# One DMA queue for loads and stores in turns, with 12 slots instead of 23

## The chip, the cores and the metric

The kernel runs on one core of one Trainium2 chip. The metric is the device time of one execution in microseconds (us). Engines are named as in the profile: PE is TensorE, DVE is VectorE, ACT is ScalarE, POOL is GpSimd, SP is SyncE; SPq and ACTq are the DMA queues that SyncE and ScalarE issue to.

## The reference

There are 128 samples. Each sample `b` is a matrix of 128 channels by 1024 time steps in float32, and it has a subject, a number from 0 to 7. Each subject has a 128 x 128 weight matrix. The sample is multiplied by the matrix of its subject, and the product is added to the sample:

```python
def reference(x, itok_B_0_7, L0_cond_weights):     # x: (128, 128, 1024), weights: (8, 128, 128)
    w = L0_cond_weights[itok_B_0_7]                # one (128, 128) matrix a sample
    return x + jnp.einsum('bct,bcd->bdt', x, w)
```

The samples are 67.1 MB that have to come in and 67.1 MB that have to go out.

## The kernel before

Samples are worked on in pairs (`G = 2`), so there are `NT = 64` pairs, each 1 MB. A pair lives in one slot of on-chip memory, `xs[k]`, with 128 channels on the partitions and 2 x 1024 values on each. There are `SLOTS = 23` slots; pair `i` uses slot `i % SLOTS`. The product is added to the sample in place, so a slot is loaded, changed and stored, and is free for another pair when the store has landed.

Each engine has its own list of instructions, and semaphores hold the lists together:

- SyncE first loads all weights (`w_all`), then issues the loads of all pairs in order. A load of a pair is two calls of `transfer`, one a sample (0.5 MB each), both counted by `s_load[k]`. For a slot's second and later uses it first waits for the store of the pair that was in it (`s_store[k]`). For the first use of the slots it keeps at most `LEAD = 3` pairs in flight, by waiting for the load of three pairs earlier.
- GpSimd reads the subject of a sample and copies its weight matrix out of `w_all` into one of four buffers (L158).
- TensorE waits for the load, and multiplies each sample in two halves of 512 columns into one of four PSUM buffers (L164). Three matmuls of zeros come ahead (L111).
- VectorE adds the PSUM buffer to the sample in its slot (L174), and counts `s_added`.
- ScalarE waits until both samples of a pair are added, and issues the pair's store, one transfer of 1 MB, counted by `s_store[k]`. It issues no arithmetic.

So loads and stores go through two hardware queues: `QUEUES` names one for SyncE and one for ScalarE. `transfer` is the helper that issues on either; its line is 53, which is why loads and stores carry the same line in the profile. In each queue the transfers start in the order of issue; between the queues nothing sets an order but the semaphores. At the end SyncE waits for the stores of the last `SLOTS` pairs.

Of the kernel before, what the change touches and what calls it, by code (L numbers as in the profile page):

```python
# [1 line left out]

# [4 lines left out]

F32 = mybir.dt.float32
I32 = mybir.dt.int32
ALU = mybir.AluOpType


G = 2

N = 512  # L30

SLOTS = 23

W_SLOTS = 4
P_SLOTS = 4
DMA = 16

LEAD = 3

IDLE = 3  # L40

ROWS = 4
QUEUES = {mybir.EngineType.SP: "qSPDynamicHW", mybir.EngineType.Activation: "qActDynamicHW"}


def transfer(nc, engine, out, in_):

    later, nc._always_lower_symbolic_ap = nc._always_lower_symbolic_ap, False  # L50
    ins, outs = engine.lower_ap_dma(in_), engine.lower_ap_dma(out)
    nc._always_lower_symbolic_ap = later
    return engine.add_instruction(  # L53
        mybir.InstDMACopy(
            name=nc.get_next_instruction_name(),
            engine=engine.engine,
            ins=ins,
            outs=outs,
            mode="Copy",
            cce_op=ALU.bypass,  # L60
            queue=QUEUES[engine.engine],
        )
    )


@with_exitstack
def kernel(
    ctx: ExitStack,
    tc: tile.TileContext,
    x: bass.AP,  # L70
    subjects: bass.AP,
    weights: bass.AP,
    out: bass.AP,
):
    nc = tc.nc
    B, C, T = x.shape
    S, _, D = weights.shape
    NT = B // G

    def sbuf(name, *shape, dtype=F32):  # L80
        return ctx.enter_context(nc.sbuf_tensor(name, list(shape), dtype)).ap()

    given, near, wrap, index = (
        sbuf(name, 1, B, dtype=I32) for name in ("given", "near", "wrap", "index")
    )
    w_all = sbuf("w_all", C, S, D)
    ws = [sbuf(f"w{i}", C, 1, D) for i in range(W_SLOTS)]
    zeros = sbuf("zeros", C, N)
    xs = [sbuf(f"x{i}", C, G, T) for i in range(SLOTS)]
    ps = [  # L90
        ctx.enter_context(nc.psum_tensor(f"ps{i}", [D, T], F32)).ap() for i in range(P_SLOTS)
    ]

    s_given = tc.alloc_semaphore("s_given")
    s_wall = tc.alloc_semaphore("s_wall")
    s_index = tc.alloc_semaphore("s_index")
    s_zeros = tc.alloc_semaphore("s_zeros")
    s_copied = tc.alloc_semaphore("s_copied")
    s_product = tc.alloc_semaphore("s_product")
    s_added = tc.alloc_semaphore("s_added")  # L100
    s_load = [tc.alloc_semaphore(f"s_load{i}") for i in range(SLOTS)]
    s_store = [tc.alloc_semaphore(f"s_store{i}") for i in range(SLOTS)]

    with tc.tile_critical():  # L104

        nc.scalar.dma_start(given, subjects.rearrange("(o b) -> o b", o=1)).then_inc(s_given, DMA)

        nc.vector.memset(zeros, 0.0).then_inc(s_zeros, 1)  # L108
        nc.tensor.wait_ge(s_zeros, 1)
        for _ in range(IDLE):  # L110
            nc.tensor.matmul(  # L111
                ps[P_SLOTS - 1][:, :N], zeros[:, :D], zeros, start=True, stop=True
            )

        nc.vector.wait_ge(s_given, DMA)
        nc.vector.tensor_scalar(near, given, -S, S - 1, ALU.max, ALU.min).then_inc(s_index, 1)  # L118
        nc.vector.wait_ge(s_index, 1)
        nc.vector.tensor_scalar(wrap, near, 0, S, ALU.is_lt, ALU.mult).then_inc(s_index, 1)  # L120
        nc.vector.wait_ge(s_index, 2)
        nc.vector.tensor_tensor(index, near, wrap, ALU.add).then_inc(s_index, 1)  # L122
        nc.gpsimd.wait_ge(s_index, 3)

        nc.sync.dma_start(w_all, weights.rearrange("s c d -> c s d")).then_inc(s_wall, DMA)  # L127
        for i in range(NT):
            k, turn = i % SLOTS, i // SLOTS
            if turn:  # L130
                nc.sync.wait_ge(s_store[k], DMA * turn)
            elif i >= LEAD:
                nc.sync.wait_ge(s_load[k - LEAD], DMA * G)
            for g in range(G):
                transfer(
                    nc,
                    nc.sync,
                    xs[k][:, g, :],
                    x[i * G + g].rearrange("(a r) t -> a (r t)", r=ROWS),
                ).then_inc(s_load[k], DMA)  # L140

        nc.gpsimd.wait_ge(s_wall, DMA)
        for i in range(NT):
            k, turn = i % SLOTS, i // SLOTS
            nc.tensor.wait_ge(s_load[k], DMA * G * (turn + 1))
            for g in range(G):
                b = i * G + g
                s = nc.values_load(
                    index[0:1, b : b + 1],
                    engines=[mybir.EngineType.Pool],  # L150
                    min_val=0,
                    max_val=S - 1,
                    skip_runtime_bounds_check_because="the index is clamped on the chip above",
                )
                w, p = ws[b % W_SLOTS], ps[b % P_SLOTS]
                if b >= W_SLOTS:
                    nc.gpsimd.wait_ge(s_product, b - W_SLOTS + 1)
                nc.gpsimd.tensor_copy(w, w_all[:, bass.ds(s, 1), :]).then_inc(s_copied, 1)  # L158

                nc.tensor.wait_ge(s_copied, b + 1)  # L160
                if b >= P_SLOTS:
                    nc.tensor.wait_ge(s_added, b - P_SLOTS + 1)
                for t in range(0, T, N):
                    mm = nc.tensor.matmul(  # L164
                        p[:, t : t + N],
                        w[:, 0, :],
                        xs[k][:, g, t : t + N],
                        start=True,
                        stop=True,
                    )  # L170
                mm.then_inc(s_product, 1)

                nc.vector.wait_ge(s_product, b + 1)
                nc.vector.tensor_tensor(xs[k][:, g, :], p, xs[k][:, g, :], ALU.add).then_inc(  # L174
                    s_added, 1
                )
            nc.scalar.wait_ge(s_added, (i + 1) * G)
            transfer(
                nc,
                nc.scalar,  # L180
                out[i * G : (i + 1) * G].rearrange("g d t -> d g t"),
                xs[k].rearrange("d (o g) t -> d o (g t)", o=1),
            ).then_inc(s_store[k], DMA)


        for i in range(NT - SLOTS, NT):
            nc.sync.wait_ge(s_store[i % SLOTS], DMA * (i // SLOTS + 1))


# [1 line left out]
_INS = ["x", "itok_B_0_7", "L0_cond_weights"]  # L191
_OUTS = [((128, 128, 1024), "float32")]


# [20 lines left out]
```

## Time and profile before

| | |
|---|---|
| median of 6 runs | 328.06 us (327.55 to 328.2) |
| the profiled execution | 328.06 us, its span 326.1 us |
| DMA: bytes, mean rate over the span | 134.86 MB, 414 GB/s |
| TensorE, VectorE, GpSimd busy | 74%, 48%, 12% of the span |
| mean granted TensorE clock | 0.925 |
| one load transfer, issue to landing | 11.8 us (median) |
| one store transfer, issue to landing | 41.5 us (median) |

The span is the part of the execution that the trace shows; the rest of the time lies around it. The strips of the page cut the span into 40 slices of 8.15 us, and each digit is the busy share of a slice in tenths. DMA is the mean of the core's 16 DMA engines, GB/s what they moved. A time "to landing" runs from the issue of a transfer until its semaphore is complete, and so has in it all the time for which the transfer waited in its queue.

### The profile page before, as it was taken

What the parts mean: (1) busy time and instruction counts of PE and PEld (TensorE: products, weight loads), DVE (VectorE), ACT (ScalarE), POOL (GpSimd) and SP (SyncE); (2) the same over time, 40 slices, a digit from 0 to 9 for tenths busy, and PEclk for the clock granted to TensorE, in tenths of its full rate; (3) what the DMA queues carried; (4) which work ended last, traced back from release to release, by engine and by line L of the source; (5) the groups of instructions that cost most, each with busy time, mean ns of one, the idle gap of its engine ahead of it and who ended that gap; (6) DMA issues with size and microseconds to landing.
All of it is one profiled execution on the core that took longest, in us unless ns stands there. A gap on an engine that the chain in (4) does not pass through costs nothing.

```text
span 326.1 us, 1941 instructions
## 1 busy us (share of the span) xinstructions
PE 241.5 (74%) x518; PEld 95.2 (29%) x518; DVE 158.0 (48%) x132; POOL 37.8 (12%) x132
## 2 busy tenths in 40 slices
PE   7999988988989888998898898898796876000000
PEld 2444433333333333333333333333232332000000
DVE  1666766556555565665565565666365445000000
POOL 1111111111111111111111111111011110000000
PEclk9999999999999999999999999999799999755555
DMA  7999999999999999999999999999999999999993
GB/s 267 408 414 420 422 426 423 426 424 427 425 421 427 423 425 423 425 428 423 427 424 419 425 424 428 422 419 426 423 438 423 419 423 427 425 427 425 427 425 166
DMA packets 16411, 134.86 MB, mean 414 GB/s; under 512 B 3089, under 2 KB 4114, under 8 KB 4114
## 3 DMA queue, kind: packets, MB, share of 16 engines
q1 hardware_dynamic: 7184, 67.64, 49.7%
q10 hardware_dynamic: 9218, 67.11, 49.1%
q8 instruction: 4, 0.07, 0.1%
q14 instruction: 5, 0.04, 0.0%
HBM read 67.63 MB, written 67.11 MB: 413 GB/s over the span
## 4 chain that ended last, share of the span: by engine, by line
DMA 45%; SPq 24%; another core or an unknown queue 14%; PE 1%; issue 1%; DVE 0%
DMA x<-in_x_dram 30%; SPq L53 23%; DMA out_dram<-x 15%; PE ps L164 1%; DVE x L174 0%; SPq L127 0%; SPq L211 0%; SPq L104 0%
## 5 line engine op out<-in xcount | busy, mean ns | idle before, releaser
L164 PE MATMUL ps<-x,w 128*128 128x512 f32 x512 | 236.0, 607 | 32.5 <-DMA x<-in_x_dram 32.2
L174 DVE TENSOR_TENSOR x<-ps,x 128x1024 f32<-128x1024 f32 x128 | 156.8, 1225 | 117.2 <-PE ps L164 117.2
L164 PEld LDWEIGHTS ps<-x,w 128*128 128x128 f32 x512 | 93.4, 191 | 175.9 <-issue 96.6
L158 POOL COPY w<-w_all 128x128 f32 x128 | 37.6, 294 | 228.1 <-PE ps L164 222.5
L111 PE MATMUL ps<-zeros 128*128 128x512 f32 x6 | 5.5, 1088 | 1.7 <-DVE zeros L108 1.7
L111 PEld LDWEIGHTS ps<-zeros 128*128 128x128 f32 x6 | 1.8, 328 | 3.7 <-issue 2.1
L108 DVE MEMSET zeros<- 128x512 f32 x1 | 0.5, 485 | 1.1 <-SPq L104 1.1
L118 DVE TENSOR_SCALAR near<-given 1x128 int32<-1x128 int32 x1 | 0.2, 215 | 0.6 <-DMA given<-in_itok_B_dram 0.6
L122 DVE CUSTOM_DVE_ANT_0 index<-near,wrap 1x256 uint16<-1x256 uint16 x1 | 0.3, 281 | 0.0
L120 DVE TENSOR_SCALAR wrap<-near 1x128 int32<-1x128 int32 x1 | 0.2, 216 | 0.0
L202 POOL MEMSET const-float32-0.0<- 128x1 f32 x1 | 0.1, 98 | 0.2 <-issue 0.2
L202 POOL MEMSET const-bfloat16-1.0<- 128x1 bf16 x1 | 0.1, 101 | 0.0
L202 POOL MEMSET const-uint8-127<- 128x1 uint8 x1 | 0.1, 101 | 0.0
L202 POOL MEMSET const-float32-1.0<- 128x1 f32 x1 | 0.1, 98 | 0.0
## 6 DMA issues: line engine op xcount, KB each, us to landing
x<-in_x_dram SPq DMA_DIRECT2D x128, 512.0 KB, 11.8
out_dram<-x ACTq DMA_DIRECT2D x64, 1024.0 KB, 41.5
w_all<-in_L_cond_weights_dram SPq DMA_DIRECT2D x1, 512.0 KB, 3.9
given<-in_itok_B_dram ACTq DMA_DIRECT2D x1, 0.5 KB
```

Source lines behind the costliest of these rows:

```text
L53: return engine.add_instruction(mybir.InstDMACopy(name=nc.get_next_instruction_name(), engine=engine.engine, ins=ins, outs=outs, mode="Cop ...
L108: nc.vector.memset(zeros, 0.0).then_inc(s_zeros, 1)
L111: nc.tensor.matmul(ps[P_SLOTS - 1][:, :N], zeros[:, :D], zeros, start=True, stop=True)
L118: nc.vector.tensor_scalar(near, given, -S, S - 1, ALU.max, ALU.min).then_inc(s_index, 1)
L120: nc.vector.tensor_scalar(wrap, near, 0, S, ALU.is_lt, ALU.mult).then_inc(s_index, 1)
L122: nc.vector.tensor_tensor(index, near, wrap, ALU.add).then_inc(s_index, 1)
L158: nc.gpsimd.tensor_copy(w, w_all[:, bass.ds(s, 1), :]).then_inc(s_copied, 1)
L164: mm = nc.tensor.matmul(p[:, t : t + N], w[:, 0, :], xs[k][:, g, t : t + N], start=True, stop=True,)
L174: nc.vector.tensor_tensor(xs[k][:, g, :], p, xs[k][:, g, :], ALU.add).then_inc(s_added, 1)
L202: nc = _bacc.Bacc("TRN2", target_bir_lowering=False, num_devices=1)
```

## The change

All loads and stores of samples are issued by SyncE on its one queue. The order is written out: the loads of the first six pairs, then in turns the load of pair `i + 6` and the store of pair `i`. `SLOTS` falls from 23 to 12, and `LEAD`, now the distance between load and store in this order, is 6 where the old `LEAD` was 3. The old wait that kept three loads in flight goes. Before a store SyncE waits for `s_added`, as ScalarE did. ScalarE keeps only the load of the subjects. The instructions of TensorE, VectorE and GpSimd stay as they are, in the same order.

```diff
-SLOTS = 23
+SLOTS = 12
...
-LEAD = 3
+LEAD = 6
...
-QUEUES = {mybir.EngineType.SP: "qSPDynamicHW", mybir.EngineType.Activation: "qActDynamicHW"}
+QUEUES = {mybir.EngineType.SP: "qSPDynamicHW"}
...
         nc.sync.dma_start(w_all, weights.rearrange("s c d -> c s d")).then_inc(s_wall, DMA)
-        for i in range(NT):
+
+        def load(i):
             k, turn = i % SLOTS, i // SLOTS
             if turn:
                 nc.sync.wait_ge(s_store[k], DMA * turn)
-            elif i >= LEAD:
-                nc.sync.wait_ge(s_load[k - LEAD], DMA * G)
             for g in range(G):
                 transfer(
                     nc,
                     nc.sync,
                     xs[k][:, g, :],
                     x[i * G + g].rearrange("(a r) t -> a (r t)", r=ROWS),
                 ).then_inc(s_load[k], DMA)
+
+        def store(i):
+            k = i % SLOTS
+            nc.sync.wait_ge(s_added, (i + 1) * G)
+            transfer(
+                nc,
+                nc.sync,
+                out[i * G : (i + 1) * G].rearrange("g d t -> d g t"),
+                xs[k].rearrange("d (o g) t -> d o (g t)", o=1),
+            ).then_inc(s_store[k], DMA)
+
+        for i in range(LEAD):
+            load(i)
+        for i in range(NT):
+            if i + LEAD < NT:
+                load(i + LEAD)
+            store(i)
...
-            nc.scalar.wait_ge(s_added, (i + 1) * G)
-            transfer(
-                nc,
-                nc.scalar,
-                out[i * G : (i + 1) * G].rearrange("g d t -> d g t"),
-                xs[k].rearrange("d (o g) t -> d o (g t)", o=1),
-            ).then_inc(s_store[k], DMA)
```

## The prediction

> **What bounds the kernel now.** I read the strips of the page first, since they show each resource over the whole span.
>
> ```profile
> PE   7999988988989888998898898898796876000000
> DVE  1666766556555565665565565666365445000000
> DMA  7999999999999999999999999999999999999993
> GB/s 267 408 414 420 422 426 423 426 424 427 425 421 427 423 425 423 425 428 423 427 424 419 425 424 428 422 419 426 423 438 423 419 423 427 425 427 425 427 425 166
> q1 hardware_dynamic: 7184, 67.64, 49.7%
> q10 hardware_dynamic: 9218, 67.11, 49.1%
> ```
>
> The DMA strip is full from the second slice to the last but one, and goes on for six slices in which TensorE and VectorE do nothing. q1 (SyncE's queue, the loads) and q10 (ScalarE's, the stores) together use 98.8% of 16 engines' span. So the bytes through the 16 DMA engines set the time: 134.86 MB. The change leaves the bytes as they are, so it can act in only two ways: it lets the engines run empty, or it changes the rate at which they move bytes.
>
> For the rate I asked for the busy time by stretches. After the times stand PE, PEld, DVE and POOL busy, then TensorE's clock, the DMA share and GB/s.
>
> ```profile
> 8.00:10.00 2.00, 2.00 (x5) 0.96 (x6) 0.08 (x1) 0.00 (x0) 1.00 1.02 426
> 10.00:12.50 2.50, 2.50 (x7) 1.14 (x6) 2.01 (x2) 0.59 (x2) 1.00 1.01 413
> 12.50:15.00 2.50, 2.50 (x7) 1.07 (x6) 1.59 (x2) 0.29 (x1) 1.00 0.98 400
> 15.00:17.50 2.50, 2.50 (x8) 1.06 (x7) 1.93 (x2) 0.59 (x2) 1.00 0.99 351
> 30.00:150.00 120.00, 107.44 (x235) 42.12 (x234) 71.21 (x60) 17.06 (x59) 1.00 1.01 425
> 220.00:270.00 50.00, 39.74 (x84) 15.67 (x83) 25.50 (x21) 5.88 (x20) 0.97 1.01 425
> 280.00:320.00 40.00, 0.00 (x0) 0.00 (x0) 0.00 (x0) 0.00 (x0) 0.51 1.01 426
> 320.00:324.50 4.50, 0.00 (x0) 0.00 (x0) 0.00 (x0) 0.00 (x0) 0.50 0.26 109
> ```
>
> Three regimes are to be seen. Up to about 17 us only loads move: first at 426 GB/s, then 413, then 400, with the engines nearly as busy. From 30 to 270 us loads and stores move together at 425. From 280 us only stores move, through one queue, at 426. So one queue alone can fill the engines when it carries stores; when it carries loads, it starts as fast and then falls.
>
> Last, the issuing side: how long an issue holds its engine (min, median, max in ns), and the landing of stores in the last stretch, where only they run.
>
> ```profile
> L53 SPq DMA_DIRECT2D x<-in_x_dram x128: 471/595/4167, 1.5 to 264.0; - x128
> L53 ACTq DMA_DIRECT2D out_dram<-x x64: 546/4311/8979, 12.9 to 301.8; - x64
> out_dram<-x ACTq DMA_DIRECT2D x10, 1024.0 KB, 22.6
> ```
>
> The median store issue holds ScalarE 4.3 us against a minimum of 0.55: the queue is full and the issue waits for room. 22.6 us to landing at 426 GB/s is 9.6 MB, so a queue holds some 9 stores. For the loads, between 90 and 145 us, the view of DMA issues gives 32.5 us to landing while q1 has 60.4% and q10 40.3% of the engines: 32.5 us x 424 GB/s x 0.6 = 8.3 MB.
>
> **The change part by part.** The profiled execution took 328.06 us, which is also the median of the runs, with a span of 326.1; 1.96 us lie around the span and I leave them. "L" below is the load of a slot (two transfers, 1.049 MB), "S" its store.
>
> Issue time. SyncE issues 128 loads and now 64 stores too: 128 x 0.595 + 64 x 0.546 = 111 us of 326, so SyncE has 215 us to spare, and it costs nothing while the queue stays filled. ScalarE loses 64 issues and had nothing else behind them.
>
> The added wait. SyncE now waits for s_added before each store, and behind it stand all later loads. The order is L(i+6), S(i), so between L(i) and S(i) lie six stores and six loads, 12.6 MB, 29.6 us at 425. With 8.3 MB (19.6 us) to 9.6 MB (22.6 us) queued, L(i) landed 7 to 10 us before SyncE gets to S(i). TensorE needs 3.71 us and VectorE's last add 1.23 us (both are the last pieces of the chain of waits), so 4.9 us. The margin is 2 to 5 us; if it were gone, SyncE would wait with some 8 MB still queued, and the engines would not notice.
>
> The slots. L(i+6) waits for S(i-6), with 10.5 MB, 24.7 us, between them: 2 to 5 us more than the queue holds. Here too a late wait finds the queue full. 12 slots are enough by the same sum.
>
> The pace of the compute. A slot needs 3.7 us of TensorE, and a pair L+S takes 4.94 us at 425 GB/s. In 220:270 the old kernel already runs at this pace, at a mean clock of 0.97. I price this at nothing; the cover is 1.2 us per pair, and it would be gone only if the clock stayed at half speed.
>
> The opening. The throttle on the first loads goes and 14 transfers go out at once, by about 10 us. SyncE then waits for the first two adds; ScalarE's first store went out at 12.9 us for the same reason. By then (12.9 - 4.9) us x 410 GB/s = 3.3 MB have landed of 7.3, so 4 MB, 10 us, are queued. Nothing runs empty. The dip in 15:17.5 (351 GB/s), where the second queue's first stores come in, may go: 2.5 x (1 - 351/410) = 0.36 us. Against that, loads alone last until 22 us instead of 17: 5 x (1 - 405/425) = 0.24 us. Together -0.1 us.
>
> The end. The last L is followed by seven stores, 17 us, instead of 23 stores. Stores alone run at 426 and mixed traffic at 425; 0. The engines' ragged finish (109 GB/s in 320:324.5) stays, since each engine still does the same work.
>
> The rate of turns. This is what decides. Until now each engine has both queues to draw from. Afterwards it does L, then S, then L, in one order, and since all 16 engines follow the same order they read memory nearly at the same time and then write it. The 57 pairs after the first seven loads become blocks of 2.47 us each. A block of stores is 280:320: 2.461 us. A block of loads has no row of its own in the mixed stage; its nearest rows are the opening's. From below: 426 GB/s, as in 8:10, so that a pair costs 4.923 us against 4.934 at 425 (0.6 us gained over 57). As the page's slices from 30 to 270 us lie between 419 and 438, most of them under 426, a mean of 424 is possible too, and then the gain is 57 x 0.023 = 1.3 us. From above: 400, as in 12.5:15, 2.621 us a block against 2.467, 57 x 0.154 = +8.8 us. Nothing excludes either side. I take the two rows that a 2.5 us block is nearest to, the first ones of a stretch of loads, 426 and 413, at their middle, 419.5: 2.500 us, +0.033 x 57 = +1.9 us. The engines drift apart by some us (the ragged finish shows it), so that part of the blocks will be mixed after all; this takes off perhaps a fifth, 0.4 us.
>
> Sum: 328.06 + 1.9 - 0.4 - 0.1 = 329.5 us.
>
> [...] The rows of 10:15 say that loads alone fall to between 413 and 400 GB/s. [...]
>
> **The rivals.**
>
> Faster: the blocks run at 426 and 426, since a block is over before the fall of 10:15 sets in, and the opening's dip goes. For it: 8:10 and 280:320. Against it: the engines have no second queue to turn to. Time: 328.06 - 1.3 - 0.4 = 326.4. It decides if a block of loads takes less than 2.467 us.
>
> No change: the engines drift so far apart that each moment is mixed as now, at 425: 328.0.
>
> Much slower: each turn from loads to stores costs what the first entry of stores cost, 0.36 us, as one queue cannot fetch ahead across a change of direction: 57 x 0.36 = 20 us, 348 us. Against it: the mixed stage changes direction all the time at 425 GB/s, though between two queues. A smaller cost per turn lies between this and the forecast.
>
> The change doesn't do what it says: the queue runs dry because SyncE waits for adds or slots. By the margins above it cannot unless the queue holds far less than 8 MB with both kinds in it; each pair would then add up to the 4.9 us of its compute, 57 x 4.9 = 279 us at most, and a tenth of that is 28 us, 356 us. I see no row for it.
>
> **How the numbers follow.** Six runs before lie between 327.55 and 328.2, so 0.2%, some 0.65 us, is about what a measurement can tell from no change. Forecast (load blocks pay in part or in full, 328.7 to 334): 0.45. Faster (326 to 327.4): 0.29. No change: 0.16. Much slower or dry (above 334): 0.10. Slower is 0.45 + 0.10 = 0.55. For 8 in 10 the range leaves out the much slower case and the last of the faster one: 326.2 to 334.5, where the upper end takes in three quarters of the 8.8 us. Of the forecast alone the range is 328.7 to 333.
>
> **What would show it.** Right: one hardware queue on the page with about 99%, the DMA strip full throughout, SyncE's waits for room or for s_store without a gap in the strip, stretches of the middle at 418 to 423 GB/s instead of 425, and TensorE busy in all slices up to some 305 us. Faster would be right with 426 or more in the middle stretches. The forecast is wrong in kind if the DMA strip shows eights or less in the middle (dry queue or costly turns), or if TensorE's clock stays at half and VectorE's adds come late.

## The result and the profile after

The changed kernel takes 328.84 us (median of 19 runs, 328.11 to 329.27), the kernel before 328.1 us (39 runs). The ratio is 1.0019 with a 95% interval of 1.0013 to 1.0025: slower by 0.62 us by the ratio, 0.43 to 0.82 (the two medians lie 0.74 us apart). The profiled execution took 328.40 us with a span of 326.6 us, 0.34 and 0.5 us over that of before; it is one of the faster runs of the changed kernel.

First the strips of its page, its one queue, and the line of the chain of waits by code line:

```profile
PE   6999968677777777687686686776776866867710
DVE  1566754454554554544544644545445446445420
DMA  7999999999999999999999999999999999999993
GB/s 257 417 408 420 426 417 424 432 416 431 430 415 429 428 419 427 426 419 435 420 422 432 423 420 429 424 422 429 424 422 427 423 422 430 420 428 430 415 427 136
q1 hardware_dynamic: 16400, 134.75, 98.6%
SPq L54 73%; PE ps L180 11%; DMA x<-in_x_dram 8%; DVE x L190 1%; SPq L127 0%; SPq L220 0%; SPq L105 0%
```

The DMA strip is as full as before. TensorE and VectorE are now spread over nearly the whole span instead of being done six slices early. 73% of the chain is SyncE's issues (SPq L54): its median issue takes 1.2 us and its shortest 0.58, so SyncE stands in its issues because the queue has no room, and the queue is never short of work (its packets take 98.6% of the 16 engines' span).

The stretches, with the columns as before (PE, PEld, DVE, POOL busy, clock, DMA share, GB/s):

```profile
8.00:10.00 2.00, 1.84 (x5) 0.89 (x6) 0.00 (x0) 0.00 (x0) 1.00 0.97 410
10.00:12.50 2.50, 2.50 (x7) 1.12 (x6) 1.83 (x2) 0.59 (x2) 1.00 1.01 419
12.50:15.00 2.50, 2.50 (x7) 1.14 (x6) 1.85 (x2) 0.29 (x1) 1.00 1.03 419
15.00:17.50 2.50, 2.50 (x7) 1.14 (x6) 1.68 (x2) 0.59 (x2) 1.00 1.02 413
17.50:20.00 2.50, 2.50 (x7) 1.10 (x6) 2.00 (x2) 0.29 (x1) 1.00 1.02 413
30.00:150.00 120.00, 92.58 (x203) 36.56 (x202) 61.62 (x52) 14.69 (x50) 1.00 1.01 424
220.00:270.00 50.00, 37.10 (x82) 14.47 (x81) 24.60 (x21) 5.98 (x21) 1.00 1.01 425
320.00:324.50 4.50, 0.00 (x0) 0.00 (x0) 0.00 (x0) 0.00 (x0) 0.50 0.23 95
```

The middle runs at 424 and 425 GB/s, where I had looked for 418 to 423. The dip of 15:17.5 is gone (413 instead of 351), and loads alone go on at 413 until 20 us. The last row, the ragged finish, is a little thinner: 95 instead of 109.

SyncE's issues and waits, durations in ns:

```profile
L54 SPq DMA_DIRECT2D x<-in_x_dram x128: 579/1206/3538, 1.5 to 286.5; - x128
L54 SPq DMA_DIRECT2D out_dram<-x x64: 539/1053/2597, 13.2 to 312.5; - x64
SPq L54 <- DVE x L190: 29.0, 13, 4.4
```

The added wait for s_added is real only 13 times, 29.0 us in all, at the opening and at the end; no wait for a store is listed for L54 at all. 12 slots and a lead of six are enough.

Where the 0.5 us of span lie can be read from the trace's single packets and semaphore increments. Summing the packets' bytes over time, 20 MB are through at 50.98 us before and 51.15 after, and 134 MB at 319.28 and 319.18. So 0.17 us is lost in the first 51 us and 0.27 us is won in the long middle. The last engine's last packet ends at 324.03 and 324.29 us, though: of the 16 increments of the last store's semaphore, the last comes 3.80 us after the first in the kernel before and 4.11 us after it in the changed one (called the lag of the last engine below). And from that last packet to the end of the span it takes 2.08 us before and 2.30 after. In there SyncE stands still for 0.36 us between two of its last instructions, which it does not do in the kernel before, while GpSimd's clearing of semaphores is shorter (0.243 instead of 0.355 us, with 22 of them fewer). 0.26 + 0.22 = 0.48 us is the whole difference in span, for this one pair of executions. The median of the changed kernel lies 0.44 us above the execution that was traced, and no trace shows where those 0.44 us lie.

The same packets show what becomes of the blocks. A load's packets carry 16 KB and a store's 8 KB, so it can be counted how many of the 16 engines move loads at a time. Slices of half a microsecond of the changed kernel, early and late, give:

| from, us | engines on loads, GB/s | from, us | engines on loads, GB/s |
|---|---|---|---|
| 25.0 | 15.1, 427 | 217.0 | 8.1, 426 |
| 25.5 | 16.0, 425 | 217.5 | 10.6, 427 |
| 26.0 | 15.9, 421 | 218.0 | 12.1, 425 |
| 26.5 | 16.0, 416 | 218.5 | 14.4, 426 |
| 27.0 | 10.8, 411 | 219.0 | 13.1, 425 |

Early on the engines are in step: all of them load, then all of them store, and within a single block of loads the rate falls from 427 to 411. Late they are out of step, some always storing while others load, and none of these slices falls. The lag is 0.9 us at 25 us, 2.1 us at 60 us and 3.2 us at 217 us. From 24.5 to 39.3 us (three pairs) the mean rate is 422.1 GB/s, from 60 to 300 us it is 425.3.

### The profile page after: what moved, and what is told of

Same layout as the page of the kernel before. It is cut to its first block, busy times and chain, and to the rows that moved or that the text cites. A ratio compares the mean times of both kernels' runs of the same rounds, so it can differ in the third digit from the quotient of the medians.

```text
span 326.6 us, 1936 instructions
## 1 busy us (share of the span) xinstructions
PE 239.9 (73%) x518; PEld 94.6 (29%) x518; DVE 158.0 (48%) x132; POOL 37.8 (12%) x132
## 3 DMA queue, kind: packets, MB, share of 16 engines
q1 hardware_dynamic: 16400, 134.75, 98.6%
## 4 chain that ended last, share of the span: by engine, by line
SPq 74%; PE 11%; DMA 8%; issue 2%; DVE 1%
SPq L54 73%; PE ps L180 11%; DMA x<-in_x_dram 8%; DVE x L190 1%; SPq L127 0%; SPq L220 0%; SPq L105 0%
```

## The experiments

The theories in the expectations: SLOTS, fewer slots cost time; BLOCKS, my prediction's, loads alone are slower than a mix; TURN, each change of direction in the queue costs something; END, the difference lies in the last engine's lag and after the last byte. OPENING, which comes later, is about the first loads, which stand behind the weights in one queue. Every ratio is against the kernel before, run on the same chip.

**Slots.** The kernel before with 12 slots, and the changed kernel with 23:

```diff
-SLOTS = 23
+SLOTS = 12
```

> The kernel before with 12 slots instead of 23 and nothing else changed. Theory SLOTS (the fewer slots cost the 0.6 us): 328.7 us. Theories BLOCKS (loads in step on all engines are slower), TURN (each change of direction in the queue costs something, 0.011 us by the measured difference) and END (the difference lies after the last byte and in the slowest engine's lag): 328.1 us, as before.

> The changed kernel with 23 slots instead of 12. SLOTS: 328.1 us, as the kernel before. BLOCKS, TURN, END: 328.8 us, as the changed kernel; END allows 0.1 us more, as more semaphores are cleared at the end.

Measured: two queues with 12 slots 328.1 us, ratio 1.0002 (0.9993 to 1.0011); one queue with 23 slots 328.63 us, 1.0018 (1.0009 to 1.0027). SLOTS falls: the number of slots does nothing that the intervals would show for either kernel. Of the two halves of the change only the one queue costs time.

**Longer blocks.** The one queue with 23 slots, in runs of four and of two:

```diff
         for i in range(LEAD):
             load(i)
-        for i in range(NT):
-            if i + LEAD < NT:
-                load(i + LEAD)
-            store(i)
+        for i in range(0, NT, RUN):
+            for j in range(i, i + RUN):
+                if j + LEAD < NT:
+                    load(j + LEAD)
+            for j in range(i, i + RUN):
+                store(j)
```

> The changed kernel with 23 slots, in an order of four loads, then four stores (10 us each) instead of one and one; ten loads come before the first store. BLOCKS: loads alone fall from about 425 to 410 GB/s after some 2.5 us, so each of 14 runs of loads loses 7.5 x (1 - 410/425) = 0.26 us, 3.7 us in all, and the longer opening 0.3 us: 332.8 us. TURN: 14 turns instead of 57 give back 0.5 us: 328.6 us with the opening. END: 329.1 us, by the opening alone.

> As the runs of four, but in an order of two loads, then two stores (5 us each); 23 slots; eight loads come before the first store. BLOCKS, with the rate of loads alone falling at once: 3.7 us as for runs of four, less what the drift takes, 331.5 to 332.5 us. BLOCKS, with the fall only after some 2.5 us of loads alone: half of each run of loads pays, 28 x 2.5 x (1 - 410/425) = 2.5 us and 0.1 us of opening, over the 328.6 us of the one queue with 23 slots: 331.2 us. If what the runs of four lost was not in the runs but in their opening and drift: 328.8 us.

Measured: runs of four 331.89 us, 1.0122 (1.0107 to 1.0136); runs of two 329.89 us, 1.0065 (1.0052 to 1.0078). The stretches 30:150 and 150:270, of runs of four and then of runs of two:

```profile
30.00:150.00 120.00, 96.69 (x200) 40.99 (x199) 60.59 (x51) 14.39 (x49) 0.90 1.01 419
150.00:270.00 120.00, 93.29 (x190) 39.24 (x189) 58.33 (x48) 14.12 (x48) 0.90 1.01 420
```

```profile
30.00:150.00 120.00, 95.27 (x205) 39.53 (x204) 62.21 (x51) 14.98 (x51) 0.96 1.01 421
150.00:270.00 120.00, 94.15 (x195) 38.63 (x194) 59.42 (x49) 14.51 (x49) 0.93 1.01 424
```

The engines are as busy as ever (1.01) and move less: long runs of loads are slow, as BLOCKS says. Against the one queue with 23 slots (328.63), runs of two lose 1.26 us by the medians, or 1.5 by the ratios, and runs of four 3.26 or 3.4. That is 0.04 to 0.05 us a run of two (28 runs, less 0.1 us for the opening) and 0.21 to 0.22 a run of four (14 runs, less 0.3).

The packets show why a run of four loses four to five times what a run of two does. In runs of four, at 203 us, the rate holds 426 until all 16 engines have loaded for about 1 us, then it stands at 409 to 412 until the run ends, five us later. In runs of two the 30:150 row gives 421 and the 150:270 row 424, though the order is the same throughout: the lag grows from 1.9 us at 40 us to 3.3 at 130 and 4.4 at 267, and the time in which all 16 engines load at once falls from about 23% of the first stretch to 13% of the second. So what counts is the time in which all engines load together; runs of 5 us are partly mixed by a lag of 3 to 4 us, and blocks of 2.5 us almost wholly. No run changed the lag alone, so this is read from traces and not tried by an edit.

TURN has no support left: between 20 and 134 MB, where most of the turns lie, the changed kernel was 0.27 us faster than the kernel before.

**Shorter blocks, and the same split with two queues.** The loop of the first, shortened:

```diff
-            store(i)
+            for h in range(2):
+                part(i + LEAD, h)      # one sample's load
+                store(i, h)            # half the partitions of a pair
```

> The changed kernel with loads and stores in turns of half a pair (0.5 MB): one sample's load, then the store of half the partitions of a pair, and so on. Twice the turns and 64 more transfers. TURN: another 57 turns at 0.011 us, 329.4 us. BLOCKS: a block of loads ends after 1.2 us, before the fall, so what the blocks cost goes: 328.3 to 328.6 us. END: 328.8 us.

> The kernel before with each store as two transfers of half the partitions (0.5 MB), on ScalarE's queue as before. It has the 64 more transfers of the half blocks without their order. TRANSFERS (each transfer costs its engine a little more, so the half blocks lost 1.4 us by their number): 329.5 us. TURN (the half blocks lost by the turns in the one queue): 328.1 us, as the kernel before.

Measured: half blocks 330.23 us, 1.0063 (1.0050 to 1.0076; one of its six executions took 340.4 us and is not in the ratio), and two queues with halved stores 331.42 us, 1.0116 (1.0080 to 1.0153). The halved store costs more where there are no turns than where there are twice as many, so the loss of the half blocks is no sign of TURN. Their trace says the same: the middle runs at 425 GB/s with twice the turns and 64 more transfers, and 134 MB are through within 0.2 us of the kernel before. The loss lies in the lag, 5.26 us instead of 3.80, and the last packet ends at 325.90 us. With two queues the lag is 5.18 us, and 150:270 runs at 420 besides. Why halved stores do this stayed open: both explanations that I had written down missed its size.

**The opening.**

```diff
-LEAD = 6
+LEAD = 4
```

> The changed kernel with LEAD 4 instead of 6: five loads instead of seven come before the first store, and 8.4 MB instead of 12.6 lie between a load and its store. BLOCKS: 5 us less of loads alone at 410 GB/s, 0.2 us less: 328.6 us. DRY (the queue holds too little once SyncE waits 4.9 us for each pair's compute): above 329.5 us, with gaps in the DMA strip.

Measured: 328.66 us, 1.0012 (1.0002 to 1.0022), as BLOCKS said, but its distance from the changed kernel is smaller than the intervals, so it decides nothing there. It does show the cover of the added wait at work. SyncE's wait and the stretches:

```profile
SPq L54 <- DVE x L190: 193.7, 64, 5.4
30.00:150.00 120.00, 89.04 (x193) 34.51 (x193) 59.17 (x49) 14.10 (x48) 1.00 1.01 424
150.00:270.00 120.00, 89.28 (x195) 34.71 (x194) 58.79 (x48) 14.11 (x48) 1.00 1.01 425
```

SyncE now waits before each of the 64 stores, 193.7 us in all, and the engines still run at 424 and 425 GB/s: while it waits, the queue still has work.

**The end.** The last waits for stores moved off SyncE, in the one queue and, as a control, in the kernel before:

```diff
         for i in range(NT - SLOTS, NT):
-            nc.sync.wait_ge(s_store[i % SLOTS], DMA * (i // SLOTS + 1))
+            nc.scalar.wait_ge(s_store[i % SLOTS], DMA * (i // SLOTS + 1))
```

> The changed kernel with the last 12 waits for stores moved from SyncE to ScalarE, so that SyncE's program ends early and its last instructions are fetched long before the end. END: the pause of 0.36 us after the last store goes, 328.4 us. OPENING: 328.8 us, as the changed kernel.

> The kernel before, two queues, with its last 23 waits for stores moved from SyncE to ScalarE. If the 0.66 us that the same edit took off the one queue is what SyncE's program costs at the end of the one queue alone: 328.1 us, as the kernel before, or 0.2 us less as the last store's landing is seen by another engine. If the edit saves as much with two queues (the end is the same in both, and the one queue's loss lies elsewhere): 327.5 us.

Measured: the one queue 328.18 us, 1.0000 (0.9989 to 1.0010); the kernel before 327.79 us, 0.9994 (0.9985 to 1.0003). From the last packet to the end of the span it now takes 1.73 us (2.30 in the changed kernel) and 1.88 us (2.08 in the kernel before). The edit brings the one queue level with the kernel before, about 0.6 us less, and takes 0.2 us off the two queues. The 0.4 us between these two savings would be what SyncE's program costs the one queue alone, but each ratio is uncertain by about 0.3 us, so that isn't shown. In the one execution traced the last packet even ends later, at 324.64 us.

To see whether the pause depends on where SyncE's program stands, I made it 64 waits longer:

```diff
+            nc.sync.wait_ge(s_load[k], DMA * G * (i // SLOTS + 1))
             nc.sync.wait_ge(s_added, (i + 1) * G)
```

> The changed kernel with one wait more ahead of each store on SyncE, for the load of the same slot, which the wait for its adds already implies. It waits for nothing, but makes SyncE's program 64 waits longer. If the pause is an accident of where SyncE's program stands when it reaches its end: the pause moves away from the end or to another place in it, 328.2 to 328.5 us. If it belongs to the one queue however long the program is: 328.8 us, with the same pause of 0.36 us.

Measured: 328.93 us, 1.0030 (1.0019 to 1.0041). The time went against the expectation and the trace with it: the pause is gone (1.94 us from the last packet to the end), but the last engine lags 5.64 us behind the first at the last stores instead of 4.11, and its last packet ends at 325.56 us. The pause comes and goes with the program, and the time doesn't follow it: it is in the traces of LEAD 4 and of the weights on ScalarE, below, and not in that of the one queue with 23 slots, which is as slow (328.63). What all six traces of this order with the queue on SyncE share is a late end of the last store: its last increment comes at 324.70 to 325.96 us, against 324.43 in the kernel before and 324.60 and 324.79 in its variants with 12 slots and with moved waits. Each of these is one execution. The lag isn't constant from one kernel to another, while the bytes moved by all engines together nearly are: 134 MB are through at 319.17 us here.

**The weights, and the queue on ScalarE.**

```diff
-        nc.sync.dma_start(w_all, ...)
+        nc.scalar.dma_start(w_all, ...)
```

> The changed kernel (one queue on SyncE) with only the load of all weights moved from SyncE to ScalarE. OPENING (the queue on ScalarE won because the first loads of samples do not stand behind the weights in one queue): about 1 us less than the changed kernel, 327.8 us. END (it won by the pause at the end of SyncE's program and by a shorter lag of the last engine): 328.8 us, unless the shorter program moves the pause.

Measured: 328.68 us, 1.0021 (1.0012 to 1.0031): nothing, and the pause is there, 0.35 us and one instruction later. OPENING falls. With the whole order of loads and stores issued by ScalarE instead:

> The changed kernel with its one queue on ScalarE instead of SyncE: the same order, waits and slots. END (part of the 0.6 us is SyncE's longer program, which pauses 0.36 us between two instructions after the last store): 328.4 to 328.5 us. If the difference belongs to the one queue and its order: 328.8 us, as the changed kernel.

> The one queue on ScalarE with its last 12 waits on ScalarE too, so that SyncE issues nothing but the weights. If the pause belongs to SyncE's program alone, moving the waits changes little: 327.1 to 327.3 us. If any engine that issues all transfers and then ends the kernel pays such a pause, 0.3 to 0.6 us more: 327.6 to 327.9 us.

Measured: 327.27 us, 0.9972 (0.9961 to 0.9982), and with the last waits on ScalarE too 326.92 us, 0.9966 (0.9954 to 0.9978). Both beat the kernel before and the changed one; the second has the lowest median of all, though the intervals of the two overlap. Stretches of the first:

```profile
30.00:150.00 120.00, 93.73 (x203) 37.13 (x202) 61.55 (x51) 14.99 (x51) 0.99 1.01 424
150.00:270.00 120.00, 89.31 (x195) 34.76 (x194) 59.30 (x49) 14.34 (x49) 1.00 1.01 425
320.00:324.50 4.50, 0.00 (x0) 0.00 (x0) 0.00 (x0) 0.00 (x0) 0.50 0.24 102
```

The middle is the same, 424 and 425. The gain is where END puts it: no pause (1.93 and 1.74 us from the last packet to the end), and a last packet at 323.82 and 323.49 us, with a lag of 3.75 and 3.64 us. The gain is larger than I had expected, and why the lag is shorter was not shown.

Two queues with the engines exchanged, and pairs loaded by one transfer on the ScalarE queue:

```diff
-            for g in range(G):
-                transfer(nc, nc.scalar, xs[k][:, g, :], x[i * G + g].rearrange("(a r) t -> a (r t)", r=ROWS))
+            transfer(nc, nc.scalar, xs[k], x[i * G : (i + 1) * G].rearrange("g d t -> d g t"))
```

> The kernel before, two queues and 23 slots, with the engines exchanged: loads on ScalarE, stores and the last waits on SyncE. OPENING: the loads no longer stand behind the weights, so this gains what the queue on ScalarE gained over the changed kernel or a part of it, 327.1 to 327.6 us. If only the one queue gains from ScalarE: 328.1 us, as the kernel before.

> The one queue on ScalarE with each pair loaded by one transfer (1 MB, rows of 4 KB) in place of two of 0.5 MB (rows of 16 KB): 64 transfers fewer. TRANSFERS (64 more cost 1.4 us in the half blocks): 325.9 us. If the shorter rows cost 2.5 ns more for each 8 KB, as stores of 8 KB at 311 ns stand to half a load of 16 KB at 616 ns: 64 pairs x 8 rows an engine x 3 ns = 1.5 us more, which cancels it: 327.3 us.

Measured: exchanged 327.64 us, 0.9987 (0.9978 to 0.9996), a third to a half of the gain, between the two expectations; pair loads 327.0 us, 0.9973 (0.9963 to 0.9982), no better than the one queue on ScalarE. In the trace of the pair loads two things cancel: 134 MB are through at 319.86 us, 0.65 us later than with rows of 16 KB, but the last engine lags only 2.35 us, and its last packet ends at 323.21 us.

## Why the prediction was right or wrong

It named the direction, slower, and the time lies in its range, but +1.44 us were forecast and +0.62 measured, and the sign came out by another way than the one I gave.

**The step that failed is the drift, which I let take off "perhaps a fifth, 0.4 us".** The price of a block was right as long as the engines are in step: I put it at 419.5 GB/s, and the blocks at 25 and at 30 us (2.5 us each) run at 420.0 and 420.4. A pair then loses 0.037 us (422.1 against 425.3 GB/s), where I had 0.033. But I multiplied that by all 57 pairs. By 60 us the engines are 2.1 us apart, which is nearly a block, and from there on the rate is 425.3: each moment is mixed, as it was with two queues. In bytes over time the turns in step cost 0.12 us between 10 and 20 MB, and the middle as a whole was 0.27 us faster. So the drift takes off nearly the whole 1.9 us. That the lag is the reason is read from the traces, in which the slow slices of the load blocks go as it grows; no run held the engines in step.

The rows that I priced from are coarse. The view counts a packet whole in the window in which it starts, as the DMA shares of 1.02 and 0.98 beside 426 and 400 show. By the packets' own times the three windows have 421, 416 and 410 GB/s; this moves the middle of the first two only from 419.5 to 418, but the fall from 426 to 400 is really one from 421 to 410. Where all 16 engines go on loading, the rate stands at 409 to 412 GB/s (the runs of four at 204 to 209 us). The blocks that are mixed do not fall to it: in the changed kernel the slices from 217 to 219.5 us run at 425 to 427.

**The second failed step is the end, which I priced at 0.** I left the 1.96 us around the span and the ragged finish as they were. In the profile the last engine's later end and SyncE's program after it gave +0.48 us. The experiments confirm the place, a last store that ends late, but not the cause: the pause in SyncE's program isn't needed for the loss, and why the last engine ends later with the queue on SyncE and earlier with it on ScalarE stays open. So it is luck that the forecast has the right sign. With the drift rightly sized and the end at nothing, I would have forecast no change.

**Right were** the steps that say why the queue stays full: SyncE's issue time costs nothing (it stands in its issues because the queue is full), the waits for adds and slots are covered (at LEAD 4 even 193.7 us of them), 12 slots are enough, the compute keeps pace, and the two rivals of costly turns and of a dry queue do not happen. That one queue cannot fetch ahead across a change of direction was a supposition of mine, which no run shows: between 20 and 134 MB, with most of the turns in it, the changed kernel gains 0.27 us. The opening was put at -0.1 us. The dip of 15:17.5 went as foreseen and gave back 0.33 us between 5 and 6 MB, and the longer stretch of loads alone took 0.28 again up to 10 MB. With 0.10 us that the traced execution was already behind at 5 MB, that makes +0.05. The dip is not what I took it for, though: in the kernel before no store's packet starts ahead of 17.45 us, so it lies in loads alone, and its cause was not shown.

Of the rivals, "no change" was right in its mechanism: the engines drift apart until each moment is mixed as before, at 425 GB/s.

Loads and stores on two issuing engines or on one makes no difference in the middle here: with a queue that is never empty, one queue moves 424 and 425 GB/s (30:150 and 150:270) and two move 425 and 424. The whole time is a little longer with one queue on SyncE (1.0019) and a little shorter with one on ScalarE (0.9972).

## What to carry to other kernels

When the DMA engines are full in every slice, neither the number of queues nor of slots mattered here, as one queue held more work than any wait in front of it lasted (a median of 20.2 us from issue to landing in the changed kernel, against single waits of 4.4 us at most); what the order could still change was the length of a run in one direction. Price a block by the time in which all DMA engines are in it together: here they drifted 2 to 4 us apart, against blocks of 2.5 us, and that mixed the blocks by itself. Below half a percent, look at the end: how far the slowest DMA engine lags behind, and what the issuing engine's program does after the last transfer.

## What the runs showed of the hardware

- Loads alone on all 16 engines fall from 426 or 427 GB/s to 409 to 412 within 1 to 2 us (the changed kernel at 25 to 27.5 us, the runs of four at 203 to 209 us); stores alone keep 426 for 40 us (the kernel before, 280:320).
- A queue holds some 8 to 10 MB of these transfers before an issue stands still. This is an estimate from times to landing: 22.6 us at 426 GB/s for the stores of the kernel before, 20.2 us (median) at 424 GB/s in the changed one.
- The 16 engines end 2.35 to 5.6 us apart, in kernels whose engines together move 134 MB within 0.9 us of each other (319.06 to 319.94 us; the kernels with longer runs or halved stores left aside). In the changed kernel the lag is 0.9 us at 25 us and 2.1 us at 60 us; in between a packet of 16 KB that is no sample's (instructions) takes 1.06 us at 42.2 us. From 143 us on it grows by another 0.06 us or so with each pair, to 4.1 us. That the packet caused the first step, and why the lag goes on growing, is inferred or open; no run tried it.
